# A two-layer mixer and experts kernel: DMA-dependent instructions pinned to program order, one power for two norms

## The chip, the cores and the metric

The kernel runs on one core of a Trainium2 chip. The metric is the device time of one execution in microseconds (us), taken as the median of several runs; lower is better. One execution was also recorded by the hardware profiler, and its records are called the trace here. Engines are named as in the profile: PE is TensorE (matmul), PEld its weight loads, DVE is VectorE, ACT is ScalarE, POOL is GpSimd, and SP is SyncE, which only issues DMAs here.

## What is computed

Input is x of 4 batches x 512 tokens x 256 channels, in f32, and the weights of two layers. Each layer is an attention-like mixer and a mixture of experts, each in a residual with a layer norm ahead and behind:

```python
x = x + _layernorm(_L0_attn_ref(_layernorm(x), ...))   # state space mixer + feed forward
x = x + _layernorm(_L0_ffn_ref(_layernorm(x), ...))    # 8 experts, top 2
x = x + _layernorm(_L1_attn_ref(_layernorm(x), ...))   # diagonal recurrence
x = x + _layernorm(_L1_ffn_ref(_layernorm(x), ...))    # 8 small experts + shared expert
```

The parts that the change touches, cut from the reference:

```python
# layer 0 mixer: a layer norm, then at once an RMS norm of its result
h = rmsnorm(hidden_states, norm1_w)
h = mixer(h, ...) + residual
# layer 0 experts: top 2 of 8 for each token
top_vals, top_idx = jax.lax.top_k(x_flat @ w_router, 2)
probs = jax.nn.softmax(top_vals, axis=-1)
h = jnp.square(jax.nn.relu(jnp.einsum('nc,ecd->ned', x_flat, w_fc)))
y = jnp.einsum('ned,edc->nec', h, w_proj)
out = jnp.einsum('nec,ne->nc', y, w_tok)
# layer 1 mixer: a recurrence along the 512 tokens
a = jnp.exp(dt[..., None] * A)
u = dt[..., None] * B * X
s = _diag_ssm_scan(a, u)          # s[t] = a[t] * s[t-1] + u[t]
y = C * s + D * X
```

For the mixer's norms: with m and v a row's mean and variance, the layer norm is h = (x - m) r with r = (v + eps)^(-1/2). Its mean square is v r r, so the RMS norm multiplies h by (v r r + eps)^(-1/2). The product of both factors is (v (1 + eps) + eps eps)^(-1/2), applied to x - m.

## The kernel before

Tokens lie on the 128 partitions, so a batch is 4 chunks of 128 tokens by 256 channels. The work of layer 0's mixer is a loop over 4 batches and, in each, over 8 groups `g` of the state heads. In a group TensorE projects B and C for the next group (`load_pair`, line 495 is its matmul, line 178 its convolution on DVE, line 176 the bias on ACT), and computes scores (`scores`: matmul L655, exponential L658, matmul L663, product L666, triangular select L669 on POOL). `first` prepares the next batch: its norms, the projection of `dt` (copied out at L596), the decays `al` (L603, used by the matmul L612) and `Mv`. `second` prepares one half of the heads: it copies rows of `Mv` into `St` by 24 small DMAs on SP (L533) and uses `selE` in the matmul L545. The loads of the next groups' weights (L485, tiles `wg` of 256 KB) are on SP as well.

Beside this loop run generators: `layer0(b)` holds the feed forward, the routing (`experts0_in`), the experts (`experts0_out`) and the return (`experts0_back`) of a batch whose mixer is done. Their `yield` values are estimates of TensorE time, of other engines' time and of a wait; the class `Side` uses them to decide when the next step is written into the program. After the fourth mixer the rest is written by a similar planner that takes in layer 1 as well.

The experts of a batch work on 15 tiles of 128 rows sorted by expert. The normed rows are written to a DRAM tensor `XD`. For tile t POOL issues two indirect DMAs in `fetch`: `xr` gathers 128 token rows out of `XD` (L401), `wx` gathers the weights of the tile's expert (L404, 5 buffers each). `three` runs three stages of different tiles: transpose of `xr` (L412) and its copy (L414), the first matmul (L419) with relu (L422) and square (L423), the second matmul (L427) with its copy (L430), which is written to the DRAM tensor `YS` (L431) by a DMA on ACT's queue. In `experts0_back` POOL gathers each token's two rows out of `YS` (L450, 8 DMAs a batch into `h` and `yg`), ACT scales the first by its probability (L454), and DVE adds the second, scaled (L455).

Layer 1's mixer (`mixer1_in`, `mixer1_out`) turns its step sizes `dts` into rows (`by_row`: DRAM tensor `dD`, L229 on SP), and reads them back spread over 128 partitions as `db` (8 DMAs, L1029 on SP). Then for four groups of channels POOL multiplies (`uu`, L1033), ACT takes the decay's exponential (L1034) and scales X (L1035), and DVE runs the recurrence (L1037) and the sums behind it.

The program is not issued as it is written. A scheduler orders each engine's instructions by its own estimate of when they will be ready, within the dependencies; so an instruction written late may be issued early, or the other way round. Nothing in this kernel keeps two instructions of an engine in the written order unless they depend on each other. All waits are semaphores; an instruction that waits holds all that stands behind it in its engine's order.

Of the kernel before, what the change touches and what calls it, by code (L numbers as in the profile page):

```python
# [8 lines left out]
F32 = mybir.dt.float32  # L9
BF16 = mybir.dt.bfloat16  # L10
I32 = mybir.dt.int32
AF = mybir.ActivationFunctionType
ALU = mybir.AluOpType
# [3 lines left out]
B, L, DM = 4, 512, 256  # L17
P = 128
NC = L // P
NH = 32  # L20
NG = 8
EPS = 1e-5
# [15 lines left out]
def tile_layers(  # L38
# [26 lines left out]
    nc = tc.nc  # L65
    V, S, G, T = nc.vector, nc.scalar, nc.gpsimd, nc.tensor

    base = ctx.enter_context(tc.tile_pool(name="base", bufs=1))
    small = ctx.enter_context(tc.tile_pool(name="small", bufs=2))

# [12 lines left out]
    xs = []  # L83
# [12 lines left out]
    make_identity(nc, ident)  # L96
    identb = base.tile([P, P], BF16, tag="identb", name="identb")
    V.tensor_copy(identb, ident)
    nhalf = base.tile([P, NC], F32, tag="nhalf", name="nhalf")
    G.memset(nhalf, -0.5)  # L100
    rev = base.tile([P, 8], F32, tag="rev", name="rev")
    for i in range(8):
# [288 lines left out]
    def experts0_out(b, t, slack=1.2):  # L391

        token, wrow = t.token, t.wrow
        x, y = XD[b % 2], YS[b % 2]
        ws, xr, hx = {}, {}, {}

        def fetch(t):

            if t < NT:
                xr[t] = wl.tile([P, DM], F32, tag="xr", name="xr", bufs=5)  # L400
                G.indirect_dma_start(out=xr[t], out_offset=None, in_=x,  # L401
                                     in_offset=bass.IndirectOffsetOnAxis(ap=token[:, t : t + 1], axis=0))
                ws[t] = wst.tile([P, 4 * DM], F32, tag="wx", name="wx", bufs=5)
                G.indirect_dma_start(out=ws[t], out_offset=None, in_=w_exp,  # L404
                                     in_offset=bass.IndirectOffsetOnAxis(ap=wrow[:, t : t + 1], axis=0))

        def three(t):

            p = ps("dc", 2)
            if t + 2 < NT:  # L410
                for k in range(2):
                    T.transpose(p[:, k * P : (k + 1) * P], xr[t + 2][:, k * P : (k + 1) * P], ident)  # L412
                hx[t + 2] = wl.tile([P, L], F32, tag="hT", name="hx", bufs=5)
                S.copy(hx[t + 2][:, : 2 * P], p[:, : 2 * P])  # L414
            if 0 <= t + 1 < NT:
                w, h = ws[t + 1], hx[t + 1]
                for d in range(2):
                    for k in range(2):
                        T.matmul(p[:, L + d * P : L + (d + 1) * P], w[:, k * DM + d * P : k * DM + (d + 1) * P],  # L419
                                 h[:, k * P : (k + 1) * P], start=(k == 0), stop=(k == 1))  # L420
                h = h[:, 2 * P :]
                S.activation(h, p[:, L : L + 2 * P], AF.Relu)  # L422
                V.tensor_tensor(h, h, h, ALU.mult)  # L423
            if t >= 1:
                w, h = ws[t - 1], hx[t - 1]
                for d in range(2):
                    T.matmul(p[:, 2 * P : 2 * P + DM], h[:, (2 + d) * P : (3 + d) * P],  # L427
                             w[:, (2 + d) * DM : (3 + d) * DM], start=(d == 0), stop=(d == 1))
                yr = wl.tile([P, L], F32, tag="th", name="yr", bufs=2)
                S.copy(yr[:, :DM], p[:, 2 * P : 2 * P + DM])  # L430
                nc.scalar.dma_start(out=y[(t - 1) * P : t * P, :], in_=yr[:, :DM])  # L431

        for t in range(3):
            fetch(t)
        yield 0.0, 0.0, 5.5
        for t in range(-2, NT + 1):
            three(t)
            fetch(t + 3 if t >= 0 else NT)
            yield 0.3 * (t < NT - 2) + 1.1 * (-2 < t < NT - 1) + 1.1 * (t > 0), 0.4, slack

    def experts0_back(b, t, gap=1.0):

        y, rsb, (p1, p2) = YS[b % 2], h1s[b], t.p
        yield 0.0, 0.0, 3.0 + gap
        yg = wl.tile([P, NC, DM], F32, tag="v", name="yg", bufs=1)
        for c in range(NC + 2):
            if c < NC:
                for i in range(2):
                    j = i * NC + c
                    G.indirect_dma_start(out=(rsb, yg)[i][:, c, :], out_offset=None, in_=y,  # L450
                                         in_offset=bass.IndirectOffsetOnAxis(ap=t.place[:, j : j + 1], axis=0))
            if c > 1:
                r = rsb[:, c - 2, :]
                S.activation(r, r, AF.Copy, scale=p1[:, c - 2 : c - 1])  # L454
                V.scalar_tensor_tensor(r, yg[:, c - 2, :], p2[:, c - 2 : c - 1], r, ALU.mult, ALU.add)  # L455
            yield 0.0, 0.6, gap
        add_layernorm(b, [rsb[:, c, :] for c in range(NC)], "a")
        yield 0.0, 4.2, 2.5
# [12 lines left out]
    with ExitStack() as c1:  # L471
# [93 lines left out]
        def first(t):  # L565

            x = xs[t.b]
            h0 = h1s[t.b] = base.tile([P, NC, DM], F32, tag="h", name="h", bufs=3)

            mv = stats(x)  # L570
            r = rsqrt(mv[:, :, 1], "rs")
            q = small.tile([P, NC], F32, tag="q", name="q")
            V.tensor_tensor(q, mv[:, :, 1], r, ALU.mult)
            V.tensor_tensor(q, q, r, ALU.mult)
            r2 = rsqrt(q, "rq")
            V.tensor_tensor(r2, r2, r, ALU.mult)
            us = []
            for c in range(NC):
                u = wk.tile([P, DM], F32, tag="u", name="u", bufs=4)
# [214 lines left out]
            G.memset(z, 0.0)  # L794
            eA.append(z)

        for b in range(1, B):
            nc.sync.dma_start(out=xs[b], in_=x_in[b].rearrange("(c p) d -> p c d", p=P))

        order = [(k, m) for k in range(2) for m in range(4)]  # L800
        nxt = [Pair(), Pair()]
# [4 lines left out]
        St = []  # L806
        for k in range(2):
            z = w0.tile([P, 8, P], BF16, tag=f"St{k}", name=f"St{k}")
            V.tensor_tensor(z, pen.unsqueeze(1).to_broadcast([P, 8, P]),
                            named[:, k * 8 : k * 8 + 8].unsqueeze(2).to_broadcast([P, 8, P]), ALU.add)  # L810
            St.append(z)

        selE = w0.tile([P, 2, P], BF16, tag="selE", name="selE")
        for e in range(2):
            for k in range(2):
                V.tensor_copy(selE[:, k, :].rearrange("r (i e m p) -> r i e m p", e=2, m=4, p=8)[:, :, e],
                              named[:, k * 8 : k * 8 + 8].rearrange("r (i m) -> r i m", m=4)
                              .unsqueeze(3).to_broadcast([P, 2, 4, 8]))
        for e in range(2):
            o = (1 - e) * 64  # L820
            G.memset(selE[o : o + 64].rearrange("r k (i e m p) -> r (k i) e (m p)", e=2, m=4, p=8)[:, :, e], 0.0)
# [9 lines left out]
        for b in range(B):  # L831
            ahead = batch(b + 1) if b + 1 < B else None
            aside = second(t, 1)
            for g, (k, m) in enumerate(order):
# [42 lines left out]
                if m == 3:  # L877
# [4 lines left out]
                    G.tensor_tensor(gT[:, P:], gT[:, P:], ebT[:, P:], ALU.add)  # L882
                    G.tensor_tensor(gT, gT, t.zT[k], ALU.mult)
                side.go(3.0, b)
                if g >= 3 and ahead:
                    if g == 3:
                        aside = first(ahead)
                    for _ in range(2):
                        next(aside, None)
                    side.go(2.5, b)  # L890
# [132 lines left out]
    def mixer1_out(b, t):  # L1023
# [6 lines left out]
                                  in_=t.dD[2 * m + i : 2 * m + i + 1, :].to_broadcast([64, L]))  # L1030
        for m in range(4):
            s = wk.tile([P, L], F32, tag="uu", name="uu", bufs=2)
            G.tensor_tensor(s, a[:, m, :], X[:, m, :], ALU.mult)  # L1033
            S.activation(a[:, m, :], a[:, m, :], AF.Exp, scale=An[:, m : m + 1])  # L1034
            S.activation(X[:, m, :], X[:, m, :], AF.Copy, scale=D1[:, m : m + 1])  # L1035
            if m == 0:
                yield 0.0, 0.0, 2.0  # L1037
# [233 lines left out]
```

## Time and profile before

| | us |
|---|---|
| three runs | 1321.13, 1323.87, 1330.15 |
| median | 1323.87 |
| the profiled execution | 1329.84 |
| its span (first to last instruction) | 1328.1 |

Busy time in some stretches of the trace, and the clock that was granted to TensorE:

| stretch (us) | PE busy | PE clock |
|---|---|---|
| 0 to 14 | 0.27 | 1.00 |
| 14 to 30 | 10.99 | 0.89 |
| 500 to 515 | 9.15 of 15 | 0.77 |
| 805 to 820 | 11.70 of 15 | 0.94 |
| 1048 to 1076 | 19.01 of 28 | 0.91 |
| 1100 to 1110 | 4.22 of 10 | 0.75 |

A line of a timeline has start, duration, engine, source line and operation, the tile written and those read, the shapes, and in square brackets the idle time of the engine ahead of it with what ended that idle time. The line of a stretch gives its bounds and length, then the busy time of PE, PEld, DVE, ACT and POOL with the number of instructions, then the granted clock, the share of time in which the DMA engines were busy, and GB/s. Line numbers are those of the kernel before; in the changed one the same statements stand 2 to 4 lines lower.

### The profile page before, as it was taken

The numbers are of one execution on the slowest core, as the hardware profiler recorded it, in microseconds if no ns is written. First come the engines' busy times: TensorE is split into PE (matmuls) and PEld (weight loads), VectorE is DVE, ScalarE is ACT, GpSimd is POOL, SyncE is SP. The second block draws the span as 40 slices with busy tenths as digits, with TensorE's granted clock in tenths as the row PEclk, the third lists the DMA queues.
The fourth block names the chain that finished last, engine by engine and source line by source line (L and its number), as shares of the span: only waits on it lengthen the run. The fifth ranks groups of instructions, "written<-read, shape, count | busy, mean of one in ns | idle before, by whom it ended". The sixth has DMA issues, their size and how long they took to land.

```text
span 1328.1 us, 18538 instructions
## 1 busy us (share of the span) xinstructions
PE 1153.0 (87%) x6896; PEld 719.5 (54%) x6896; DVE 794.2 (60%) x1754; ACT 543.5 (41%) x980; POOL 326.9 (25%) x415
## 2 busy tenths in 40 slices
PE   4688988999889997899988998898998778888776
PEld 2354545455556663556655764554576666555543
DVE  5656565656755457656766465736437336576765
ACT  2343342333334334343323443324236355486644
POOL 5010201100243413210114423200333552220110
PEclk8899899999879998899989998998998888888878
DMA  5010001010132522101014533060435554110100
GB/s 183 19 34 24 26 18 33 18 52 17 48 116 82 171 89 75 33 17 53 17 34 143 162 113 112 1 179 16 151 103 156 176 153 139 42 40 9 41 16 24
DMA packets 76153, 97.41 MB, mean 73 GB/s; under 512 B 11008, under 2 KB 62208, under 8 KB 76064
## 3 DMA queue, kind: packets, MB, share of 16 engines
q0 software_dynamic: 13488, 45.10, 11.6%
q1 hardware_dynamic: 53936, 43.26, 10.8%
q10 hardware_dynamic: 8640, 7.87, 1.7%
q8 instruction: 55, 0.90, 0.3%
q14 instruction: 34, 0.28, 0.1%
HBM read 85.25 MB, written 12.12 MB: 73 GB/s over the span
## 4 chain that ended last, share of the span: by engine, by line
PE 64%; DVE 15%; POOL 6%; issue 5%; ACT 5%; DMA 4%; another core or an unknown queue 0%; SPq 0%; POOLq 0%; ACTq 0%; DVEq 0%
PE ps_pj L495 16%; PE ps_dc L280 6%; PE ps_dc L663 4%; PE ps_pj L679 3%; PE ps_dc L427 3%; PE ps_dc L294 3%; DVE BT L178 3%; PE ps_dc L419 3%; PE ps_yA L869 3%; PE ps_dc L940 2%; PE ps_b L1007 2%; PE ps_pj L646 2%; PE ps_yB L874 2%; DVE st L111 2%; DVE sc L666 2%
## 5 line engine op out<-in xcount | busy, mean ns | idle before, releaser
L495 PE MATMUL ps_pj<-uT,wg 128*128 128x512 f32 x512 | 268.5, 652 | 18.6 <-ACT sc L658 5.8
L178 DVE SCALAR_TENSOR_TENSOR BT<-ps_pj,col,BT 128x511 f32<-128x511 f32 (+2 forms) x192 | 143.1, 746 | 107.8 <-ACT BT L176 100.7
L669 POOL TENSOR_SCALAR_AFFINE_SELECT sc<-sc 128x1024 f32<-128x1024 f32 x64 | 70.2, 1096 | 434.2 <-DVE sc L666 406.5
L495 PEld LDWEIGHTS ps_pj<-uT,wg 128*128 128x128 f32 x512 | 94.3, 202 | 114.0 <-issue 81.9
L178 DVE SCALAR_TENSOR_TENSOR CT<-ps_pj,col,CT 128x511 f32<-128x511 f32 (+2 forms) x192 | 142.4, 742 | 20.8 <-ACT CT L176 11.7
L663 PE MATMUL ps_dc<-CT,BT 64*128 64x128 f32 x1024 | 95.6, 302 | 9.0 <-DVE sc L666 5.4
L663 PEld LDWEIGHTS ps_dc<-CT,BT 64*128 64x128 f32 x1024 | 75.1, 196 | 48.6 <-issue 34.2
L176 ACT ACTIVATE CT<-ps_pj,col 128x512 f32<-128x512 f32 x64 | 49.7, 777 | 122.4 <-PE ps_pj L495 117.2
L666 DVE TENSOR_TENSOR sc<-sc,ps_dc 128x1024 f32<-128x1024 f32 x64 | 77.7, 1215 | 30.3 <-PE ps_dc L663 20.2
L404 POOL DMA_INDIRECT wx<-in_w_exp_dram,wrow x60 | 61.2, 1020 | 112.5 <-PE ps_dc L427 70.2
L280 PE MATMUL ps_dc<-vT,wf 128*128 128x512 f32 x192 | 87.0, 595 | 0.3 <-ACT vT L137 0.3
L176 ACT ACTIVATE BT<-ps_pj,col 128x512 f32<-128x512 f32 x64 | 49.7, 777 | 90.9 <-PE ps_pj L495 87.8
L658 ACT ACTIVATE sc<-ps_dc 128x1024 f32<-128x1024 f32 x64 | 65.7, 1026 | 46.3 <-PE ps_dc L655 44.2
L427 PE MATMUL ps_dc<-wx,hx 128*128 128x256 f32 x240 | 69.8, 417 | 11.9 <-ACT hx L422 8.4
L419 PEld LDWEIGHTS ps_dc<-hx,wx 128*128 128x128 f32 x480 | 66.6, 204 | 20.4 <-issue 10.4
L419 PE MATMUL ps_dc<-hx,wx 128*128 128x128 f32 x480 | 70.2, 291 | 6.2 <-DMA wx<-in_w_exp_dram,wrow 4.3
L401 POOL DMA_INDIRECT xr<-XD,token x60 | 58.2, 971 | 69.2 <-PE ps_dc L412 53.8
L427 PEld LDWEIGHTS ps_dc<-wx,hx 128*128 128x128 f32 x240 | 46.1, 205 | 33.0 <-ACT hx L422 17.9
L423 DVE TENSOR_TENSOR hx<-hx 128x256 f32<-128x256 f32 x60 | 28.0, 466 | 54.0 <-ACT hx L422 48.1
L869 PE MATMUL ps_yA<-sc,xz 128*32 128x128 f32 x1024 | 52.2, 284 | 7.9 <-POOL sc L669 4.4
L280 PEld LDWEIGHTS ps_dc<-vT,wf 128*128 128x128 f32 x192 | 35.5, 190 | 41.0 <-issue 38.3
L679 PEld LDWEIGHTS ps_pj<-xd,bt 128*128 128x128 f32 x384 | 48.6, 200 | 12.9 <-issue 11.3
(311 smaller groups left out, 2014.5 us busy)
## 6 DMA issues: line engine op xcount, KB each, us to landing
wg<-in_w_in_dram SPq DMA_DIRECT2D x64, 256.0 KB
YS<-yr ACTq DMA_DIRECT2D x60, 128.0 KB
wf<-in_w_gate_dram SPq DMA_DIRECT2D x32, 128.0 KB
wf<-in_w_up_dram SPq DMA_DIRECT2D x32, 128.0 KB
wf<-in_w_down_dram SPq DMA_DIRECT2D x32, 128.0 KB
db<-dD SPq DMA_DIRECT2D x32, 128.0 KB
St<-Mv SPq DMA_DIRECT2D x192, 2.0 KB
x<-in_x_dram SPq DMA_DIRECT2D x4, 512.0 KB
```

What stands on the lines that cost most here:

```text
L176: S.activation(dst, p, AF.Identity, bias=bias, scale=w(3))
L178: V.scalar_tensor_tensor(dst[:, s:], p[:, : L - s], w(3 - s), dst[:, s:], ALU.mult, ALU.add)
L280: T.matmul(p, we[:, i * 2 + k, :], vT[:, k, :], start=(k == 0), stop=(k == 1))
L419: T.matmul(p[:, L + d * P : L + (d + 1) * P], w[:, k * DM + d * P : k * DM + (d + 1) * P], h[:, k * P : (k + 1) * P], start=(k == 0), stop ...
L427: T.matmul(p[:, 2 * P : 2 * P + DM], h[:, (2 + d) * P : (3 + d) * P], w[:, (2 + d) * DM : (3 + d) * DM], start=(d == 0), stop=(d == 1))
L495: T.matmul(p, w[:, k, :], uT[:, k, :], start=(k == 0), stop=(k == 1))
L658: S.activation(sc, df, AF.Exp)
L663: T.matmul(cb[:, e * L + c * P : e * L + (c + 1) * P], of.BT[e * 64 : (e + 1) * 64, c * P : (c + 1) * P], of.CT[e * 64 : (e + 1) * 64, c * ...
L666: V.tensor_tensor(sc, sc, cb, ALU.mult)
L669: G.affine_select(out=scv, in_=scv, compare_op=ALU.is_ge, fill=0.0, base=0, pattern=[[0, 2 * NC], [1, P]], channel_multiplier=-1)
L679: T.matmul(p[:, i * 48 : (i + 1) * 48].rearrange("p (e d c) -> p c e d", d=8, c=3)[:, c], pairs[i].bt[:, c, :], t.xd[k][:, c].rearrange("p ...
L869: T.matmul(yA[q * 32 : (q + 1) * 32, c * P : (c + 1) * P], xz[k][:, c, q, m, :], scs[q // 2][:, (q % 2) * L + c * P : (q % 2) * L + (c + 1 ...
```

## The change

A function of the scheduler, bound to the name `later`, pins an instruction in its engine's order behind the one written just before it on that engine. It makes no wait. It is applied to the expert gathers (L401, L404), the return gathers (L450), the scaling and the sum of the returned rows (L454, L455), the `uu` product and the exponential of layer 1 (L1033, L1034), and the making of `St` and `selE` (L809, L816). The loads of x for batches 1 to 3 move from ahead of the loop into the group with g == 1 of the batch before, pinned too. `first` uses one power over both norms' factors instead of two powers in turn. Two estimates of waits are changed: in `experts0_out` a yield of 5.5 becomes one of 2.0 after each of three fetches and one more, and in `experts0_back` 3.0 + gap becomes 3.0 + 2.0 * gap.

```diff
+    later = tc.keep_in_program_order
...
-    nhalf = base.tile([P, NC], F32, tag="nhalf", name="nhalf")
+    nhalf = base.tile([P, 2 * NC], F32, tag="nhalf", name="nhalf")
...
                 xr[t] = wl.tile([P, DM], F32, tag="xr", name="xr", bufs=5)
-                G.indirect_dma_start(out=xr[t], out_offset=None, in_=x,
-                                     in_offset=bass.IndirectOffsetOnAxis(ap=token[:, t : t + 1], axis=0))
+                later(G.indirect_dma_start(out=xr[t], out_offset=None, in_=x,
+                                           in_offset=bass.IndirectOffsetOnAxis(ap=token[:, t : t + 1], axis=0)))
                 ws[t] = wst.tile([P, 4 * DM], F32, tag="wx", name="wx", bufs=5)
-                G.indirect_dma_start(out=ws[t], out_offset=None, in_=w_exp,
-                                     in_offset=bass.IndirectOffsetOnAxis(ap=wrow[:, t : t + 1], axis=0))
+                later(G.indirect_dma_start(out=ws[t], out_offset=None, in_=w_exp,
+                                           in_offset=bass.IndirectOffsetOnAxis(ap=wrow[:, t : t + 1], axis=0)))
...
         for t in range(3):
             fetch(t)
-        yield 0.0, 0.0, 5.5
+            yield 0.0, 0.0, 2.0
+        yield 0.0, 0.0, 2.0
...
-        yield 0.0, 0.0, 3.0 + gap
+        yield 0.0, 0.0, 3.0 + 2.0 * gap
...
-                    G.indirect_dma_start(out=(rsb, yg)[i][:, c, :], out_offset=None, in_=y,
-                                         in_offset=bass.IndirectOffsetOnAxis(ap=t.place[:, j : j + 1], axis=0))
+                    later(G.indirect_dma_start(out=(rsb, yg)[i][:, c, :], out_offset=None, in_=y,
+                                               in_offset=bass.IndirectOffsetOnAxis(ap=t.place[:, j : j + 1], axis=0)))
             if c > 1:
                 r = rsb[:, c - 2, :]
-                S.activation(r, r, AF.Copy, scale=p1[:, c - 2 : c - 1])
-                V.scalar_tensor_tensor(r, yg[:, c - 2, :], p2[:, c - 2 : c - 1], r, ALU.mult, ALU.add)
+                later(S.activation(r, r, AF.Copy, scale=p1[:, c - 2 : c - 1]))
+                later(V.scalar_tensor_tensor(r, yg[:, c - 2, :], p2[:, c - 2 : c - 1], r, ALU.mult, ALU.add))
...
             mv = stats(x)
-            r = rsqrt(mv[:, :, 1], "rs")
-            q = small.tile([P, NC], F32, tag="q", name="q")
-            V.tensor_tensor(q, mv[:, :, 1], r, ALU.mult)
-            V.tensor_tensor(q, q, r, ALU.mult)
-            r2 = rsqrt(q, "rq")
-            V.tensor_tensor(r2, r2, r, ALU.mult)
+            ve = small.tile([P, 2, NC], F32, tag="rse2", name="ve")
+            V.tensor_scalar_add(ve[:, 0], mv[:, :, 1], EPS)
+            V.tensor_scalar(ve[:, 1], mv[:, :, 1], 1.0 + EPS, EPS * EPS, ALU.mult, ALU.add)
+            rr = small.tile([P, 2, NC], F32, tag="rs2", name="rr")
+            G.tensor_tensor(rr.rearrange("p a c -> p (a c)"), ve.rearrange("p a c -> p (a c)"), nhalf, ALU.pow)
+            r, r2 = rr[:, 0], rr[:, 1]
...
-        for b in range(1, B):
-            nc.sync.dma_start(out=xs[b], in_=x_in[b].rearrange("(c p) d -> p c d", p=P))
...
-            V.tensor_tensor(z, pen.unsqueeze(1).to_broadcast([P, 8, P]),
-                            named[:, k * 8 : k * 8 + 8].unsqueeze(2).to_broadcast([P, 8, P]), ALU.add)
+            later(V.tensor_tensor(z, pen.unsqueeze(1).to_broadcast([P, 8, P]),
+                            named[:, k * 8 : k * 8 + 8].unsqueeze(2).to_broadcast([P, 8, P]), ALU.add))
...
-                V.tensor_copy(selE[:, k, :].rearrange("r (i e m p) -> r i e m p", e=2, m=4, p=8)[:, :, e],
+                later(V.tensor_copy(selE[:, k, :].rearrange("r (i e m p) -> r i e m p", e=2, m=4, p=8)[:, :, e],
                               named[:, k * 8 : k * 8 + 8].rearrange("r (i m) -> r i m", m=4)
-                              .unsqueeze(3).to_broadcast([P, 2, 4, 8]))
+                              .unsqueeze(3).to_broadcast([P, 2, 4, 8])))
...
                 side.go(3.0, b)
+                if g == 1 and ahead:
+                    later(nc.sync.dma_start(out=xs[b + 1], in_=x_in[b + 1].rearrange("(c p) d -> p c d", p=P)))
...
             s = wk.tile([P, L], F32, tag="uu", name="uu", bufs=2)
-            G.tensor_tensor(s, a[:, m, :], X[:, m, :], ALU.mult)
-            S.activation(a[:, m, :], a[:, m, :], AF.Exp, scale=An[:, m : m + 1])
+            later(G.tensor_tensor(s, a[:, m, :], X[:, m, :], ALU.mult))
+            later(S.activation(a[:, m, :], a[:, m, :], AF.Exp, scale=An[:, m : m + 1]))
```

## The prediction

> **What bounds the kernel now.** Four views were read in this order: the summary with its chain of waits, the stretches (busy time by window), the timeline of TensorE's gaps, and the timelines of the engines that those gaps name. The summary and the chain first.
>
> ```profile
> PE 1153.0 (87%) x6896; PEld 719.5 (54%) x6896; DVE 794.2 (60%) x1754; ACT 543.5 (41%) x980; POOL 326.9 (25%) x415
> PE 64%; DVE 15%; POOL 6%; issue 5%; ACT 5%; DMA 4%; another core or an unknown queue 0%; SPq 0%; POOLq 0%; ACTq 0%; DVEq 0%
> ```
>
> TensorE is busy 1153.0 of 1328.1 us. The change takes no matmul away, so all it can win or lose is in TensorE's 175 idle us and in its clock. By windows the idle time is about 33 us in 0 to 100, 64 us in 100 to 900 and 79 us in 900 to 1328.1. The head:
>
> ```profile
> 7.18 1.03 POOL L121 TENSOR_TENSOR rs<-rse,nhalf 128x4 f32<-128x4 f32 x1 [5.38 <-DVE identb L98]
> 11.59 1.05 POOL L121 TENSOR_TENSOR rq<-rqe,nhalf 128x4 f32<-128x4 f32 x1
> 13.73 2.13 PE L133 MATMUL ps_pj<-ident,u 128*128 128x128 f32 x8 [13.73 <-POOL part L765]
> 19.66 2.36 DVE L809 TENSOR_TENSOR St<-pen,named 128x1024 bf16<-128x1024 f32 x2 [5.05 <-POOL named L773]
> 23.49 0.26 DVE L596 COPY dt<-ps_pj 128x128 f32<-128x128 f32 x1
> 27.58 0.77 PE L612 MATMUL ps_pj<-al,tri_u 128*128 128x128 f32 x2 [4.29 <-DVE al L603]
> ```
>
> Two powers with constants between them stand before the first transpose. Then VectorE sits 5.05 us in front of St, and dt, whose product was ready about 19.8 (15.99 + 3.84), is read at 23.49; L612 pays 4.29 us. The middle, when batch 0's expert rows come back:
>
> ```profile
> 494.91 0.95 POOL L450 DMA_INDIRECT h<-YS,place  x1 [8.31 <-DMA YS<-yr]
> 498.26 0.51 ACT L454 ACTIVATE h<-h,p 128x256 f32<-128x256 f32 x1 [2.23 <-DMA h<-YS,place]
> 501.18 0.51 ACT L454 ACTIVATE h<-h,p 128x256 f32<-128x256 f32 x1 [2.41 <-DMA h<-YS,place]
> 504.04 0.51 ACT L454 ACTIVATE h<-h,p 128x256 f32<-128x256 f32 x1 [2.35 <-DMA h<-YS,place]
> 506.54 3.78 PE L495 MATMUL ps_pj<-uT,wg 128*128 128x512 f32 x4 [5.85 <-ACT sc L658]
> ...
> 500.00:515.00 15.00, 9.15 (x61) 4.34 (x62) 7.33 (x13) 5.90 (x9) 6.13 (x6) 0.77 0.34 103
> ```
>
> ACT's queue holds exponentials and convolutions behind scalings that wait for gathers 1.25 us apart. TensorE loses 5.85 us, and the granted clock is 0.77 in the stretch. In the tail the same gathers and the decays of layer 1 meet:
>
> ```profile
> 1041.50 0.77 PE L419 MATMUL ps_dc<-hx,wx 128*128 128x128 f32 x2 [4.35 <-DMA wx<-in_w_exp_dram,wrow]
> 1058.14 1.02 POOL L450 DMA_INDIRECT h<-YS,place  x1 [1.37 <-issue]
> 1074.21 0.60 PE L412 MATMUL ps_dc<-ident,xr 128*128 128x128 f32 x2 [2.82 <-ACT yr L430]
> 1104.60 1.28 ACT L1034 ACT_TABLE_LOAD   x1 [5.31 <-DMA db<-dD]
> 1107.02 2.08 PE L427 MATMUL ps_dc<-wx,hx 128*128 128x256 f32 x4 [5.78 <-ACT hx L422]
> 1048.00:1076.00 28.00, 19.01 (x86) 12.63 (x84) 11.81 (x46) 8.94 (x23) 20.25 (x22) 0.91 0.54 165
> ```
>
> The last row says that TensorE idles 8.99 of the 28 us in which batch 2's rows come back. Eight xr gathers of batch 3 were issued there before the first L450, so it has tiles to work on while POOL gathers back.
>
> **The change, part by part.** [...]I compared the planned order of each engine before and after.
>
> *One power (L121, L573 to L576).* Per batch one POOL power of 128x8 for two of 128x4 (1.03 and 1.05 us), two small VectorE operations for five (0.14 to 0.25 us each). Beyond batch 0 this is about 3 x (1.0 POOL + 0.5 DVE) under TensorE's work: nothing. In batch 0, u no longer waits for the 11.59 power. The one power runs at 7.2 to 8.2, and u's first row comes ahead of h, so the first transpose follows at about 8.7: 5.0 us earlier. A power over twice the columns is not in the trace; it is bounded by 1.03 (no dearer) and 2.1 (as two), and I take 1.05[...].
>
> *St and selE pinned.* They now stand behind the second convolution of BT, so dt is read at once: al falls from 27.2 to about 17.9 and L612 from 27.58 to about 18.4 (-9.2). Then something else is late: St 2.36 + selE 0.49 + POOL's selE memset 0.48, now at about 34.4 to 37.9, in front of L545 (45.24 before, about 38.0 after). That makes the gain 7.2 us there. St's DMAs (24 in 16.49 us, before from 39.01) would end at about 52, and L655, 64.73 before, needs them at about 57.5: hidden by 5 us. I take -7.5 for the head (-10 to -5).
>
> *Loads of x1 to x3 moved into the loop.* Three DMAs of 512 KB. On SP the load of x3 stands behind St's 24 issues and two weight loads and comes up at about 487 by the place of its neighbours; VectorE needs it at about 496. x0 took 7.20 + 2.27 us; a load that waits longer than about 8 us stalls VectorE's statistics and the convolutions behind them. For x1 the margin is about 17 us. Batch 1's statistics and norm (about 4.7 us of VectorE at 22 to 34, where TensorE waited anyway) move to about 93 to 110, where convolutions want VectorE. Between 0 (hidden) and +4.7 (all shown) I take +1, VectorE being 60% busy.
>
> *Gathers and sums pinned, batches 0 and 1.* L450's gathers now have more than four selects (L669) between them, and the L454/L455 sums stand three or more groups of convolutions later in ACT's queue, when the rows have landed. The 5.85 goes, and so do 4.98 us of VectorE's wait. The clock belongs to it: the trace has it at half from 514.9 to 521.7, 6.8 us, which is 3.4 us of work. The Trainium skill, in "TensorE: Matmul & The Clock Gate", section "HAM oscillation — how this bites in real kernels", asks for no TensorE gap above about 3.4 us; its Part 1 puts the warm-up at about one such window, so 1.7 us of lost work, where this trace shows 3.4. With the page the removed gap is worth 7.6, with the trace 9.2. What is then late is the select that now stands behind a gather's issue (1.25 us each, at most four): -2. Batch 0 thus gives about -7. Batch 1 had 3.30 (817.87) and 2.10 (822.77), and half clock from 828.9 to 839.2; I take -3, as part of its clock loss follows other gaps. On the other side, a wx gather pinned in place can hold selects: POOL waits 70.2 us before L404 in all, but TensorE waited for selects only 4.4 us (L869). I leave that in the range (+0 to +4). Middle: -10 (-15 to -2).
>
> *The same pins in the tail.* Here they speak against. In the planned order only three xr gathers of batch 3 (against eight) now stand before L450's eight gathers, and the second decay product L1033 before and the third after them. POOL takes its instructions in the planned order, so tile 3 waits for all of it. Counted from the last L427 of batch 2 (1049.66): the first L450 comes at +4.5 to +8.6 (before +8.5), eight gathers take 10.0, L1033 1.26, the xr gather 0.95 and its landing 2 to 2.5 us, so tile 3 can start at +19.5 to +23. TensorE's queue up to its transpose holds L412 x6, L419 x8 and two L1043 groups, about 6 us. That is a stall of 13 to 17, and about 6 more on the next tiles whose gathers follow at 1.25 us each. Before, 8.99 us were lost there: net +11. The gap is far above the page's 3.4 us, which makes the half clock another +3 by the trace (six other stretches after gaps of 4 to 6 us stand at 0.70 to 0.85). Against that, the wx of the last tile of batch 2 no longer stands behind four xr: -3 of the 4.35 at 1041.50. L1034's exponentials, pinned, come between other functions: 62 table loads by the planned order against 59, and 7 more in the part after the last expert tile. At 1.28 us that is 9 us on an ACT that is 41% busy; the chain has ACT at 5%; I take +2 (0 to +6). The waits at 1104 to 1107 stay, since the DMA of dD comes first, but a product no longer held by other gathers may give -5: all of 5.78 would be its bound, 0 the other; it lies nearest to a queue that merely shifts, so -3. Some of the stall is covered too, since layer 1's convolutions can float up; I take -2. Tail: 11 + 3 - 3 + 2 - 3 - 2 = +8 (-6 to +20).
>
> *Estimated costs (fetch, back).* They only shape the order already counted.
>
> **Sum.** -7.5 + 1 - 10 + 8 = -8.5 us. The profiled execution is 1329.84 us, its span 1328.1, so 1.7 us lie around it; it stands 0.45% above the median of the three runs, 1323.87. On the median -8.5 gives about 1315.5, so 1316.
>
> **The rivals.** (a) The tail stall is covered: ACT and VectorE have a backlog after 1050, TensorE lost about 9 there before, and it catches up. Tail -2, head and middle -18: 1304, faster. For it: 79 idle us in the tail belong to a chain of small steps, which a stall of TensorE doesn't lengthen. Against it: all chains of batches 2 and 3 pass those same POOL gathers.
>
> (b) The pinned gathers win over the rest, slower. One mechanism: L450 in front of L401 on POOL at batch 2's return. If tile 3 comes at +23 and the next tiles run at POOL's pace, with every gap above 3.4 us at half clock, the tail loses 17 + 10 + 8 - 9 = 26, and batch 3's chain, the last, is late by all of it; with the middle at only -2: -7.5 + 1 - 2 + 26 = +17.5, about 1341. It decides from a net tail loss above about 30 us where the middle is worth its -10, above 22 where it is -2.
>
> (c) The pins don't bind, since an instruction pinned behind one that floats floats along; the load of x2 does so in the planned order and stays early. Then only the head is left, with the tail unchanged: 1324 - 6 = 1318, within 1%.
>
> (d) x3 comes late behind SP's queue: VectorE waits some 5 to 10 us at 496, and the middle's gain goes: 1323.
>
> **How the numbers follow.** The sum with a tail of +4 to +14: 0.30; (a) 0.32; (b) 0.20; (c) 0.08; (d) 0.10. One per cent, about what a measurement of this kernel tells from no change, is 13.2 us: faster is below 1310.6, slower above 1337.1. Most of (a) and a little of the sum are faster: 0.33. Most of (b), and a little of (d), with an unseen stall, is slower: 0.21. The rest, 0.46, lies within. The range, 1298 to 1339, reaches down to (a) with the full head and middle, and up to most of (b). The likeliest case alone has 1308 to 1324.
>
> **What would show it.** First matmul near 8.7; dt near 15 and L612 near 18.4; no L454 wait of 2 us near 500 and a clock above 0.95 at 500 to 515; one TensorE gap of 13 to 17 us before an L412 group (two to four lines lower in the new file) just after batch 2's last L427, with a clock near 0.75 behind it; some 62 table loads. I am wrong if that gap is under 8 us, if the head doesn't move, or if new gaps stand in 100 to 900 with POOL's gathers as their releaser.

## The result, and the profile after

The changed kernel takes 1358.57 us (median of 5 runs, 1353.55 to 1360.84) against 1327.11 us for the kernel before beside it: a ratio of 1.0239, with a 95% interval of 1.0203 to 1.0274. It is 31.5 us slower, where 8 us faster was predicted and 1339 us was the upper end of the range. Its profiled execution has a span of 1356.8 us, 28.7 us more than before.

First the head, in the timelines of TensorE and VectorE after (lines of the new file: L135 is the first transpose, L600 the copy of dt, L616 the product behind `al`).

```profile
9.66 2.18 PE L135 MATMUL ps_pj<-ident,u 128*128 128x128 f32 x8 [9.66 <-DVE u L127]
...
15.85 0.29 DVE L600 COPY dt<-ps_pj 128x128 f32<-128x128 f32 x1 [3.78 <-PE ps_pj L597]
...
19.24 0.77 PE L616 MATMUL ps_pj<-al,tri_u 128*128 128x128 f32 x2
```

The first matmul comes 4.1 us earlier, L616 8.3 us earlier and without its wait. Then busy time by stretch, for those that answer to the ones of before; the changed kernel first:

```profile
500.00:515.00 15.00, 15.00 (x123) 8.58 (x122) 8.16 (x17) 7.03 (x9) 9.54 (x9) 1.00 0.32 97
850.00:900.00 50.00, 40.39 (x109) 21.86 (x108) 15.39 (x39) 13.85 (x25) 3.81 (x5) 0.79 0.44 114
1048.00:1076.00 28.00, 12.07 (x47) 9.39 (x47) 12.82 (x22) 9.03 (x18) 17.48 (x17) 0.70 0.45 129
1140.00:1225.00 85.00, 63.18 (x268) 39.05 (x267) 62.06 (x166) 58.77 (x106) 20.53 (x19) 0.85 0.11 34
```

and two of them before, which were not shown:

```profile
850.00:900.00 50.00, 48.30 (x246) 28.35 (x246) 21.48 (x45) 13.89 (x27) 8.22 (x9) 1.00 0.45 119
1140.00:1225.00 85.00, 70.23 (x310) 41.82 (x309) 58.63 (x188) 56.98 (x107) 17.82 (x17) 0.84 0.09 28
```

The middle is cured: in 500 to 515 TensorE is busy without a break, at full clock. Three later stretches are worse, with 7.9, 6.9 and 7.1 us less TensorE time, and in the first two the clock falls from 1.00 and 0.91 to 0.79 and 0.70. The gaps of the first two, in TensorE's timeline after:

```profile
870.07 2.04 PE L1003 MATMUL ps_b<-xT,w1i 128*128 128x512 f32 x2 [7.56 <-DMA w1i<-in_w_in_dram]
...
1054.64 0.69 PE L414 MATMUL ps_dc<-ident,xr 128*128 128x128 f32 x2 [4.40 <-ACT yr L432]
...
1071.63 0.66 PE L414 MATMUL ps_dc<-ident,xr 128*128 128x128 f32 x2 [10.41 <-DMA xr<-XD,token]
```

The last pair is the stall that the prediction named (13 to 17 us in one gap; 14.8 in two in the trace). The first is new: layer 1's first projection (L999 before, L1003 now) stands in front of 31 of batch 2's 32 gate and up matmuls (the trace counts each as two) and waits for a weight load. This place, where layer 1's work begins, is called the seam below.

More telling than the gaps is where the last expert matmul (L427 before) ends, and how long the rest takes from there to the last instruction that the timeline shows: 1132.5 and 192.9 us before, 1140.3 and 213.8 us after. (The span ends 2.7 us behind the last line of the timeline in both.) Of some 29 us, 21 are lost behind the last expert tile, where none of the gaps named in the prediction lies.

### The profile page after: what moved, and what is told of

It reads as the page before. It is cut to its first block, busy times and chain, and to the rows that moved or that the text cites. A ratio compares the mean times of both kernels' runs of the same rounds, so it can differ in the third digit from the quotient of the medians.

```text
span 1356.8 us, 18489 instructions
## 1 busy us (share of the span) xinstructions
PE 1160.9 (86%) x6896; PEld 720.5 (53%) x6896; DVE 797.4 (59%) x1742; ACT 549.3 (40%) x983; POOL 324.0 (24%) x411
## 5 line engine op out<-in xcount | busy, mean ns | idle before, releaser
L498 PE MATMUL ps_pj<-uT,wg 128*128 128x512 f32 x512 | 269.8, 657 | 11.2 <-ACT bt L652 6.9
L498 PEld LDWEIGHTS ps_pj<-uT,wg 128*128 128x128 f32 x512 | 96.2, 205 | 110.0 <-issue 85.1
L282 PE MATMUL ps_dc<-vT,wf 128*128 128x512 f32 x192 | 90.0, 613 | 0.0
L429 PE MATMUL ps_dc<-wx,hx 128*128 128x256 f32 x240 | 65.1, 396 | 2.9 <-ACT hx L424 2.2
L652 ACT COPY bt<-ps_pj 128x384 f32<-128x384 f32 x64 | 30.5, 477 | 70.6 <-PE ps_pj L650 70.1
L1047 PE MATMUL ps_o<-w1o,Gt 128*128 128x256 f32 x128 | 38.5, 453 | 19.7 <-DVE Gt L1044 19.7
```

The costliest lines, as they stand in the source:

```text
L282: T.matmul(p, we[:, i * 2 + k, :], vT[:, k, :], start=(k == 0), stop=(k == 1))
L498: T.matmul(p, w[:, k, :], uT[:, k, :], start=(k == 0), stop=(k == 1))
```

## The experiments

Four series ran, each beside the kernel before and each on one chip, which differs from series to series; e5 to e8 and the later repetition e9, e10 shared one. Which chip gave the first result is not on record. Ratios are to the kernel before of the same series. The last two columns are worked out from the traces.

| run | kernel | ratio (95%) | median us | last L427 ends | from there to the end |
|---|---|---|---|---|---|
| e1 | changed, no return pins | 1.0119 (1.0069 to 1.0169) | 1345.26 | 1125.9 | 212.4 |
| e2 | changed, no fetch pins | 1.0173 (1.0115 to 1.0231) | 1352.69 | 1132.9 | 210.2 |
| e3 | changed, no pins on gathers, sums, decays | 1.0063 (1.0039 to 1.0088) | 1335.73 | 1139.2 | 189.7 |
| e4 | as e3, old estimates | 0.9995 (0.9968 to 1.0022) | 1328.20 | 1128.4 | 192.9 |
| e5 | changed + L999 pinned | 1.0440 (1.0403 to 1.0477) | 1390.45 | 1176.7 | 209.8 |
| e6 | changed, no decay pins | 1.0262 (1.0224 to 1.0300) | 1364.68 | 1161.1 | 194.8 |
| e7 | changed, batch 3's fetch not pinned | 1.0430 (1.0386 to 1.0474) | 1388.22 | 1171.8 | 210.5 |
| e8 | fetch pins of batches 0, 1 only | 1.0133 (1.0094 to 1.0172) | 1348.83 | 1150.1 | 195.0 |
| e9 | changed, again | 1.0371 (1.0310 to 1.0431) | 1379.94 | 1161.6 | 213.8 |
| e10 | e5, again | 1.0429 (1.0373 to 1.0484) | 1390.48 | 1173.7 | 213.8 |
| e11 | before + decay pins | 1.0138 (1.0101 to 1.0174) | 1346.89 | 1123.6 | 217.5 |
| e12 | before + exponential's pin | 1.0137 (1.0104 to 1.0170) | 1349.36 | 1126.7 | 217.4 |
| e13 | before + product's pin | 1.0002 (0.9972 to 1.0032) | 1328.98 | 1126.0 | 195.9 |
| e14 | changed, no return or decay pins | 0.9986 (0.9963 to 1.0008) | 1328.42 | 1133.9 | 193.0 |
| e15 | before + return pins | 0.9934 (0.9912 to 0.9955) | 1324.26 | 1124.7 | 191.5 |
| e16 | before + fetch pins | 1.0053 (1.0028 to 1.0078) | 1339.28 | 1147.1 | 190.0 |
| e17 | changed, no exponential's pin | 1.0262 (1.0214 to 1.0309) | 1368.78 | 1167.7 | 197.3 |
| e18 | single power, St, selE; loads early | 1.0008 (0.9983 to 1.0032) | 1333.54 | 1131.7 | 192.9 |

**First series: which pins.** The theories: the loss lies at the seam of the layers (L999 in front of the feed forward), or in the tail (return gathers in front of batch 3's tiles). Edits, each in the changed kernel:

```diff
-                    later(G.indirect_dma_start(out=(rsb, yg)[i][:, c, :], out_offset=None, in_=y,
+                    G.indirect_dma_start(out=(rsb, yg)[i][:, c, :], out_offset=None, in_=y,
...
-                later(S.activation(r, r, AF.Copy, scale=p1[:, c - 2 : c - 1]))
+                S.activation(r, r, AF.Copy, scale=p1[:, c - 2 : c - 1])
```

is e1, with the sum on VectorE done in the same way, and

```diff
-                later(G.indirect_dma_start(out=xr[t], out_offset=None, in_=x,
+                G.indirect_dma_start(out=xr[t], out_offset=None, in_=x,
...
-                later(G.indirect_dma_start(out=ws[t], out_offset=None, in_=w_exp,
+                G.indirect_dma_start(out=ws[t], out_offset=None, in_=w_exp,
```

is e2. e3 does both and takes `later` from L1033 and L1034 too; e4 also puts the old estimates back.

> The changed kernel without the pins on L450, L454 and L455 (the return gathers, the scaling, the sum). Its planned order differs from that of the changed kernel at the seam of the layers: no gate or up matmul of batch 2's feed forward (L280) stands behind the first projection of layer 1 (L999), as in the kernel before, where the changed kernel has 31 behind it; batch 3's tiles still have three gathers ahead of batch 2's return gathers. Seam theory (some 10 to 17 us are lost where L999 stands in front of the feed forward and waits 7.56 us for the load of w1i): that wait goes, the middle loses its gain of some 8 us, the tail stays: 1340 to 1352 us. Rival, the tail alone (return gathers in front of tile 3's gather cost all of it): no gain at the seam, 1358 to 1368 us.

> The changed kernel without the pins on L401 and L404 (the expert gathers). Planned order: eight xr gathers of batch 3 stand ahead of batch 2's return gathers, as in the kernel before; the seam keeps L999 in front of 31 matmuls of L280. Tail theory (three gathers instead of eight leave TensorE without a tile for 10.41 us, with slower tiles behind it): the gap goes and 8 to 20 us with it: 1338 to 1350 us. Rival (the seam and the pinned decays make the loss; the gap is covered later): 1355 to 1360 us.

> The changed kernel with no pins on L401, L404, L450, L454, L455, L1033 and L1034; the single power, the moved loads of x, the pins on St and selE and the new estimates stay. Planned order: seam and number of gathers ahead as in the kernel before. If seam and tail together make the loss: 1322 to 1332 us, as before. If the moved norm work and the moved loads cost what the head gains and more: 1333 to 1342 us.

> As the run without pins on gathers, sums and decays, and with the old estimates of waits in fetch and in the return. Left of the change are the single power, the moved loads of x, and St and selE pinned. By the prediction's sum: head -7.5, moved norm work +1: 1317 to 1323 us. By the trace of the changed kernel, where the lead of 3 to 5 us at 20 to 95 us is gone by 100 to 300 us: 1325 to 1331 us.

e1 came in its first range (1345), e2 between its two (1353), so at this point both places looked guilty. e3 was 6.3 per mille above the kernel before, and the old estimates (e4) took the rest away. e4 is the surprise for the head: its lead of 8 us at L612 is worth nothing that can be measured at the end (-4.2 to +2.9 us). e1 has a second reading: it still has a gap of 10.25 us in front of a transpose of batch 3's rows (at 1058.74, waiting for `xr`).

**Second series: the two places by themselves.** e5 keeps L999 of batch 0 in its written place, which puts it behind the feed forward; e7 unpins the gathers of batch 3 alone, so that eight tiles are ahead again; e6 drops the decay pins; e8 keeps fetch pins and new estimates for batches 0 and 1 only.

```diff
-                T.matmul(p, w1i[:, k, m * P : (m + 1) * P], xT[:, k, :], start=(k == 0), stop=(k == 1))
+                i = T.matmul(p, w1i[:, k, m * P : (m + 1) * P], xT[:, k, :], start=(k == 0), stop=(k == 1))
+                if b == 0:
+                    later(i)
```

is e5; in e7 `fetch` uses, in place of `later`,

```diff
+        keep = later if b < 3 else lambda i: i
```

> The changed kernel with one more pin: the X projections of layer 1 for batch 0 (L999 of the kernel before) are kept in their written place, which puts them behind batch 2's gate and up matmuls but for the last two rows; the order around batch 3's gathers stays (three gathers ahead of the return gathers). Seam theory: the wait of 7.56 us for w1i goes, and with its half clock 8 to 13 us: 1345 to 1351 us. Rival (the loss at the seam is only work put off, made up later): within 3 us of the changed kernel, 1355 to 1361 us.

> The changed kernel without the pins on L1033 and L1034 (the decay product and its exponential). Planned order: five xr gathers of batch 3 ahead of the return gathers instead of three; the seam as in the changed kernel. If the pinned decays cost by themselves in the last 150 us (TensorE waits 4.07 and 6.52 us for Gt there in the three traces with these pins and not in the two without): 1345 to 1351 us. If only the number of gathers ahead matters: 1352 to 1356 us.

> The changed kernel with the gathers L401 and L404 of batch 3 alone unpinned. Planned order: eight xr gathers ahead of batch 2's return gathers; seam and decays as in the changed kernel. Tail theory: the gap of 10.41 us goes: 1346 to 1352 us. Rival (batch 3's gathers are not what holds the tail): 1355 to 1361 us.

> Pins on the expert gathers of batches 0 and 1 alone, new estimates for these two alone, no pins on return gathers, sums and decays; the single power, the moved loads, St and selE as in the changed kernel. Planned order: seam and gathers ahead as in the kernel before. If the gain of 8 to 10 us in 500 to 850 belongs to the gathers of batches 0 and 1 and nothing else is lost: 1316 to 1322 us, faster than before. If the lead is given back at the seam of the layers in any case: 1325 to 1331 us.

All four were far above every expectation, and the traces had a wait of VectorE that the first series didn't have. So the changed kernel and e5 were run again side by side:

> The changed kernel unaltered, once more, beside the next one. The four runs of the second series (e5 to e8) have, in the same matmul group of batch 1 near 395 us, a wait of 6.6 us of VectorE's scan L684 that neither the first series nor the changed kernel's first run has, though the planned order up to there is the same. If the wait belongs to those kernels: 1355 to 1361 us and no such wait here. If it belongs to the chip or to the session that they ran in, and this one shares it: 1375 to 1395 us with the wait.

> The kernel with the X projections of layer 1, batch 0, pinned, unaltered, once more beside the changed kernel. Seam theory: 8 to 13 us below the changed kernel of the same series, whatever that one's level is. If the kernel itself is slow: 1385 to 1393 us and the wait of 6.6 us again.

On this chip the changed kernel itself takes 1379.94 us, where it took 1358.57 at first, with the kernel before at 1330 here and 1327 there. So e5 to e8 have to be held against 1379.94, and e8, at 1348.83 with the same wait of VectorE in its trace, says little of its own parts. Then e5 and e10 are 10.5 us slower than it: curing the seam made it worse. L999's wait is gone and the transposes of batch 2's routing start at 942.21 instead of 952.32, but layer 1's batch 0 (its `by_row`, L225) comes at 1062 instead of 994, and the last expert matmul 12 us later. e7 is 8 us slower although the gap (11.10 us in e9, 10.41 at first) is gone: other waits stand in its place, in its TensorE timeline:

```profile
1086.43 0.44 PE L416 MATMUL ps_dc<-ident,xr 128*128 128x128 f32 x2 [3.11 <-ACT yr L434]
...
1104.55 3.47 PE L431 MATMUL ps_dc<-wx,hx 128*128 128x256 f32 x8 [5.03 <-ACT hx L426]
...
1129.29 1.13 PE L431 MATMUL ps_dc<-wx,hx 128*128 128x256 f32 x4 [2.80 <-ACT hx L426]
```

Neither place explains the loss. e6 was the clue: 15.3 us faster than the changed kernel on that chip, with the last expert matmul at the same place (1161.1 and 1161.6) and the whole difference behind it (194.8 and 213.8). Over all runs the last column has two groups: 190 to 197 us without the exponential's pin, 209 to 218 with it.

**Third series: the decay pins alone.** On the kernel before:

```diff
-            G.tensor_tensor(s, a[:, m, :], X[:, m, :], ALU.mult)
-            S.activation(a[:, m, :], a[:, m, :], AF.Exp, scale=An[:, m : m + 1])
+            later(G.tensor_tensor(s, a[:, m, :], X[:, m, :], ALU.mult))
+            later(S.activation(a[:, m, :], a[:, m, :], AF.Exp, scale=An[:, m : m + 1]))
```

e11 has both, e12 the second alone, e13 the first alone. e14 is the changed kernel without the return and the decay pins.

> The kernel before with the two pins on L1033 and L1034 as its only change. Decay theory: the stretch from the last expert matmul (L427) to the end grows from 193 to 209 to 215 us, the waits of the output matmul L1043 for Gt from 4 to 16 to 20 us, ACT loads 62 tables: 1342 to 1350 us. Rival (the decay pins cost only in company of the pinned gathers): 1324 to 1334 us.

> The kernel before with the pin on the exponential L1034 alone. Planned order: 62 table loads on ACT as with both pins. If ACT's order (a table load of 1.28 us between other functions, and an exponential behind the copy of X that waits for POOL) makes the loss: 1340 to 1350 us. If POOL's does: 1325 to 1333 us.

> The kernel before with the pin on the product L1033 alone. Planned order: 57 table loads. If POOL's order makes the loss: 1338 to 1350 us. If ACT's does: 1322 to 1332 us.

> The changed kernel without the return pins (L450, L454, L455) and without the decay pins (L1033, L1034); the expert gathers stay pinned. If both losses add: 193 to 196 us behind the last expert matmul and 1320 to 1328 us on a chip without VectorE's unexplained waits, 1335 to 1350 us on one with them. If the pinned expert gathers cost in the tail by themselves: more than 200 us behind the last expert matmul.

The pin on the exponential costs 1.37% (18 us), the one on the product nothing. The wait of L1043 for Gt, which e11's expectation used as a mark, is a poor one: it is 16.6 us in e13 too, at no cost. What tells is ACT's timeline for batch 2's four exponentials (L1034) and the loads of function tables (ACT_TABLE_LOAD) beside them, before:

```profile
1181.92 1.28 ACT L1034 ACT_TABLE_LOAD   x1
1183.22 0.72 ACT L1034 ACTIVATE db<-db,An 128x512 f32<-128x512 f32 x1
...
1185.40 0.73 ACT L1034 ACTIVATE db<-db,An 128x512 f32<-128x512 f32 x1
...
1186.76 1.28 ACT L1057 ACT_TABLE_LOAD   x1
...
1189.34 1.28 ACT L1034 ACT_TABLE_LOAD   x1
1190.63 0.72 ACT L1034 ACTIVATE db<-db,An 128x512 f32<-128x512 f32 x1
...
1193.33 1.28 ACT L1001 ACT_TABLE_LOAD   x1 [1.30 <-DVE X L178]
...
1197.33 1.28 ACT L1034 ACT_TABLE_LOAD   x1
1198.63 0.72 ACT L1034 ACTIVATE db<-db,An 128x512 f32<-128x512 f32 x1
```

and in e12 (the same line, L1036 there):

```profile
1187.65 0.72 ACT L1036 ACTIVATE db<-db,An 128x512 f32<-128x512 f32 x1
...
1193.29 1.07 ACT L137 COPY xT<-ps_b 128x512 f32<-128x512 f32 x2 [2.70 <-PE ps_b L135]
...
1198.96 0.78 ACT L178 ACTIVATE X<-ps_b,col 128x512 f32<-128x512 f32 x1 [2.23 <-PE ps_b L1001]
...
1201.70 1.28 ACT L1036 ACT_TABLE_LOAD   x1
1202.99 0.72 ACT L1036 ACTIVATE db<-db,An 128x512 f32<-128x512 f32 x1
1203.73 1.28 ACT L1003 ACT_TABLE_LOAD   x1
...
1210.75 1.28 ACT L1036 ACT_TABLE_LOAD   x1
1212.05 0.72 ACT L1036 ACTIVATE db<-db,An 128x512 f32<-128x512 f32 x1
1212.79 1.28 ACT L1003 ACT_TABLE_LOAD   x1
...
1219.21 1.28 ACT L1036 ACT_TABLE_LOAD   x1
1220.51 0.72 ACT L1036 ACTIVATE db<-db,An 128x512 f32<-128x512 f32 x1
1221.25 1.28 ACT L1101 ACT_TABLE_LOAD   x1
```

From the first to the last exponential it is 15.4 us before and 32.9 us with the pin. Before, the exponentials may move up past other ACT work, and the first two are 2.2 us apart; pinned, each stands behind whatever ACT work the planner had written ahead of it (transposed rows, convolution biases and SiLUs of batch 3, sigmoids of the experts). The table loads are the smaller part of the 17.5 us: six fall between the first and the last exponential against four, 2.6 us. ACT's waits there grow from 1.5 to 9.4 us, because the work in front of an exponential itself waits for TensorE, VectorE or POOL (as in the lines with 2.70 and 2.23); the rest, about 7 us, is other work. Over all, ACT loads 26 tables behind the last expert matmul, 19 before.

The spread alone is not the measure: in e13 the four exponentials take 25.0 us at no cost. What counts is when the last one comes: at 1198.63 before and 1202.69 in e13, but at 1220.51 in e12. Batch 3 follows that chain: the gate tile Gt has one buffer, so ACT's L1008 for batch 3 waits for batch 2's output matmuls. Before and then e12:

```profile
1207.36 0.60 ACT L1008 ACTIVATE Gt<-ps_b 128x512 f32<-128x512 f32 x1 [2.83 <-PE ps_o L1043]
```

```profile
1227.88 1.08 ACT L1010 ACTIVATE Gt<-ps_b 128x512 f32<-128x512 f32 x2 [4.19 <-PE ps_o L1045]
```

Batch 3's `by_row` (L225) comes at 1246 instead of 1225, 26 us behind the last exponential in both, and the end with it.

**Fourth series: the rest.** e15 and e16 put the other two groups of pins on the kernel before, by the same kind of edit; e17 takes the exponential's pin out of the changed kernel; e18 is e4 with the three loads of x put back ahead of the loop.

> The kernel before with the pins on L450, L454 and L455 as its only change. If the return pins cost by themselves what their removal gave (13 us): 1336 to 1344 us, with the stretch behind the last expert matmul at 193 to 197 us and that matmul some 10 us later. If they take the 5.85 us stall near 506 away and cost nothing elsewhere, as predicted for the middle: 1316 to 1323 us.

> The kernel before with the pins on L401 and L404 as its only change. Planned order: three xr gathers of batch 3 ahead of batch 2's return gathers instead of eight. By the prediction's step for the tail this alone costs 8 to 14 us: 1336 to 1342 us. If the gap is covered: 1322 to 1332 us.

> The changed kernel without the pin on the exponential L1034 alone. If that pin's cost adds to the rest: 16 to 20 us below the changed kernel, 1338 to 1343 us on a chip without VectorE's unexplained waits and 1359 to 1365 us on one with them, with 193 to 197 us behind the last expert matmul. If the rest grows in its place: less than 10 us below it.

> The kernel with the single power, and St and selE pinned, but the loads of x1 to x3 ahead of the loop as before, and no other part of the change. If the moved norm work takes what the head gains: 1320 to 1324 us, 4 to 8 us below the kernel before. If the lead of the head is lost in the loop in any case: 1325 to 1331 us.

The return pins alone gain 0.66% (0.45 to 0.88%): with them the stretch of the old stall reads, in e15's view by stretch,

```profile
500.00:515.00 15.00, 12.59 (x81) 6.64 (x80) 6.98 (x10) 5.47 (x7) 7.55 (x9) 0.80 0.31 95
```

12.59 us of TensorE work instead of 9.15, and ACT waits in front of none of its 16 scalings for returned rows, where it waited 25.1 us before and 10.5 us in the changed kernel. By its ratio this is the fastest kernel of the study, 8.8 us below the one before. The fetch pins alone cost 0.53% (some 7 us), less than the 8 to 14 us of the prediction's step; but e16's trace has a wait of VectorE of 6.77 us that is described in the last section, so what they cost without it is not shown. e17 and e9 ran on different chips; by their ratios the exponential's pin is worth 1.1% (14 us, between e17's two expectations) in the changed kernel, and the part behind the last expert matmul falls to 197.3. e18 shows no gain of the head either (-2.3 to +4.3 us), but its head differs: with the loads early VectorE works on batch 1's norms there, and L615 (L612 before) comes at 23.92, only 3.7 us ahead of the kernel before.

## Why the prediction was wrong

The step that is shown to have failed is in the tail: "L1034's exponentials, pinned, come between other functions: 62 table loads by the planned order against 59 ... I take +2 (0 to +6)". The planned order was read rightly (62 loads in the trace), but it was priced as three or seven loads on an engine that is 41% busy. The pin costs 18 us alone (e12). What counts is that each exponential takes its place behind batch 3's work and that work's waits, so that they come 8 to 15 us apart, in a stretch that is a chain of small steps through ACT, VectorE, POOL and TensorE, and that the next batch waits for that chain's buffer. The sum should have followed L1034 to L1043 and on to batch 3's L1008 in the planned order of ACT, as it followed dt to L612 in the head. A second step failed too: the pinned gathers and sums as a whole, the middle's -10 and the stall's 11 + 3, were to cost some 4 us. With the return pins the changed kernel is 1.2% slower than without them (1.0239 against 1.0119 in e1). Why is open.

Point by point:

- Head, -7.5. The steps came nearly as worked out: first matmul 9.66 (8.7 predicted), dt 15.85, L616 at 19.24 (18.4), then L545 late as named, at 39.15 (38.0). The power over twice the columns was mis-sized: it took 1.66 us (L579), not 1.05. That the head shortens the kernel is not shown: e4 and e18 are at 0.9995 and 1.0008. In the changed kernel the lead is gone early: of the projection matmuls (L495, L498 now) the one at 72 us before comes 2.9 us earlier and the one at 120 us 0.3 us later. Whether the moved norm work takes it is open, since e18 has half the lead from the start.
- Loads of x, +1. The "7.20 + 2.27" given for x0 are not its load: x0 was issued at 0.82, and from 7.20 on SP issued the other three loads, in 2.27 us. In the changed kernel these come at 15.47, 73.17 and 483.32, and VectorE's statistics wait for none of them.
- Middle, -10. Right in place: no break and clock 1.00 in 500 to 515, and the mixer's last projection matmul comes at 830.48 instead of 845.76, though part of that is other work put off. The return pins alone give -8.8 us (-11.7 to -6.0) over the whole kernel; that all of it comes from the middle is not shown, and e15's stretch is only partly cured. The clock term was misread: the half clock of 514.9 to 521.7 lies at 504.3 to 511.1 on the timeline's scale (that of 828.9 to 839.2 at 818.3 to 828.6). Before, by stretch:

```profile
504.30:511.10 6.80, 4.56 (x9) 1.80 (x9) 3.25 (x6) 3.33 (x6) 1.65 (x2) 0.50 0.14 39
514.90:521.70 6.80, 6.80 (x70) 4.51 (x69) 5.76 (x19) 3.67 (x5) 1.37 (x2) 1.00 0.22 72
```

So TensorE worked for only 4.56 of these 6.8 us at half clock: 2.3 us of work were lost, not 3.4, and the gap was worth 8.1 us, not 9.2.

- Return gathers in front of batch 3's tile 3. The stall came as predicted: 4.40 and 10.41 us, L450 first at 1057.35, clock 0.70 in the stretch. Its net cost of 11 + 3 us is not supported: e7 takes the gap away and is no faster, and e1 keeps a gap of 10.25 us there and takes no more (1.0119) than the exponential's pin alone (1.0137).
- Rival (b), slower at 1341 us, had the sign, but named that stall as its one mechanism. e1 and e7 speak against it as the one that decides.
- Rivals (c) and (d): the pins bind, and no stall at x3's statistics shows.

Two groups of pins make the 31.5 us. By the ratios of kernels whose traces lack VectorE's wait, the changed kernel stands at 1.0239, without the return pins at 1.0119 (e1), and without the decay pins as well at 0.9986 (e14): 1.2% and 1.3%, with the fetch pins and the new estimates still in place. These runs come from different series, so the split is rough. The second part is the exponential's pin: 18 us alone (e12), 15.3 us with the product's pin in the changed kernel (e6 against e9, one chip). Its loss lies behind the last expert matmul. The first part lies ahead of it: that matmul ends at 1140.3 in the changed kernel and at 1125.9 in e1. There the return pins come with L999 ahead of 31 matmuls and the wait of 7.56 us; but putting L999 back (e5, e10) cost 10.5 us more, so the seam is where time is seen to go, not what shortens the kernel when mended. (In e15, with the return pins alone, half of the gate and up matmuls stand ahead of it and it waits 0.35 us.)

Why the return pins turn from gain to loss stays open. The ratios point to the fetch pins as their partner. Without fetch pins, e3 with the exponential's pin would stand at 1.0063 x 1.0137 = 1.0201 as an estimate, and e2, which has the return pins too, stands at 1.0173: no loss. With the fetch pins the same step goes from 1.0119 to 1.0239. Return and fetch pins together on the kernel before, which would test it, were not run. The new estimates cost 7.5 us in e3 against e4 and nothing that shows in e14, where the fetch pins are kept.

## What to carry to other kernels

Fixing an instruction's place helped here where what stood behind it would otherwise wait for a DMA (e15), and hurt where the instruction itself stood in a chain and was put behind work that waits (e12): look at who waits for it, and at what will stand ahead of it, before pinning it. Where the largest engine is 87% busy on average, find the stretch in which it is not, and price the change there by the chain's length, not by the engine's idle time. Try the parts of such a change one at a time, and then in pairs: the group of pins that gained 0.66% alone cost about 1.2% among the others.

## What was not expected of the hardware

The same changed kernel took 1358.57 us at first and 1379.94 us in e9, with the kernel before at 1327 and 1330. In the slower trace VectorE's scan (L684 before, L688 here) starts late and names no releaser that the trace knows; VectorE's timeline there, and then in the first trace:

```profile
389.24 0.73 DVE L180 SCALAR_TENSOR_TENSOR CT<-ps_pj,col,CT 128x510 f32<-128x510 f32 x1
396.58 0.35 DVE L688 TENSOR_TENSOR_SCAN H<-eA,ps_pj 128x96 f32<-128x96 f32 x1 [6.61 <-remote]
```

```profile
391.80 0.74 DVE L180 SCALAR_TENSOR_TENSOR CT<-ps_pj,col,CT 128x510 f32<-128x510 f32 x1
393.67 0.35 DVE L688 TENSOR_TENSOR_SCAN H<-eA,ps_pj 128x96 f32<-128x96 f32 x1 [1.13 <-PE ps_pj L683]
```

The order around it is the same, and POOL issues six expert gathers in a row in both. The wait is 6.6 to 6.8 us in every kernel with pinned expert gathers on that chip and on the one of the fourth series (e5 to e10, e16, e17), and absent in the first and third series, with pinned gathers too (e1, e14). e9 has two shorter waits of the same kind behind it (3.80 and 3.60 us at the same line), 14.0 us in all, and is 21 us slower than the first run.

One thing is common to all 17 such waits in the traces: the scan starts 1.0 to 1.4 us after POOL has issued the last of a row of gathers, expert gathers at the long waits, return gathers at the short ones. In the first trace it starts in the middle of such a row. What ties VectorE to the gathers, and why only in some series, was not found; so numbers of kernels with pinned gathers are best compared within one series.
